# A four-layer convolution stack: expansion rows of layer 0 in four PSUM banks, with copies of 768 columns

## The chip, the cores and the metric

The kernel runs on one core of a Trainium2 chip. The metric is the device time of one execution in microseconds (us); lower is better. Times before a change and after it are medians of several runs.

## What is computed

Four layers are applied one after the other to `x` of shape (4, 64, 256, 256); each adds its result to its input, which is first group-normalized (`_gn`). Only layer 0 is touched:

```python
x = jnp.einsum('bchw,oc->bohw', x, w_in)             # 64 -> 384 channels: the "expansion"
xf = jnp.fft.rfft2(patches_of_8x8(x)) * fft_filter
x = jnp.fft.irfft2(xf, s=(8, 8))                     # back to the image layout
x = lax.conv_general_dilated(x, w_dw, ..., feature_group_count=C)   # 3x3 per channel
x1, x2 = jnp.split(x, 2, axis=1)
x = jax.nn.gelu(x1, approximate=False) * x2          # 384 -> 192
return jnp.einsum('bchw,oc->bohw', x, w_out)         # 192 -> 64: the "projection"
```

The filter and the 3x3 convolution together are one linear map for each channel, from the 64 pixels of a patch and some of its neighbours to 64 output pixels.

## The kernel before

Layer 0 works on 12 blocks `p` (three for each of four images). A block has up to 12 rows of patches; a row of patches is 8 image rows by 32 patches. Four blocks have 12 steps of expansion for each channel block, eight have 11, since the image's edge leaves a row out.

For each block a loop over four channel blocks `kb` (48 channels of each of the two halves `x1` and `x2`) does this:

1. **Expansion** (`expand`, lines 459 to 490). One step makes 16 patches of each of two rows (or one whole row). The stationary operand is the pixels, the moving one the 96 weights `win`, so that pixels come out on partitions and channels along the free dimension. If `pairs` is true, one matmul takes two patches: 128 pixels on 128 partitions, 16 matmuls a step in the program (L470). If not, each patch has a matmul of its own on 64 partitions, 32 a step (L476); the weights are then taken in such an order that the channels land on the half of the partitions where they belong. The hardware records show two matmuls for each one in the program.
2. **Copies of the expansion** into the tile `u` in SBUF (L486 for pairs, L488 to L490 for single patches). A step has two PSUM tiles of two banks each, `s` = 0 and 1. ScalarE (ACT) empties tile 0, VectorE (DVE) tile 1. Pairs need four copies of 64 partitions x 384 elements from each tile, single patches three.
3. **The convolution** (`own` L523, `beside` L539) from `u` into PSUM tiles `pc`, then GELU on ScalarE (L546), the product on VectorE (L547) and a store of `g` to DRAM. It has twelve groups `g` for a `kb`, in pairs.
4. At four of these pairs, the first among them, `unit()` does a part of the **projection** of the block before (`project`, matmuls L632 and L639, additions on VectorE L648 to L653), which comes between the last matmul of the expansion and the first of `own`.

`banks(name)` hands out PSUM: four tags of two banks each, in turn, for everything in layer 0. A step of expansion takes two of the four tags, so the matmuls of step t+2 need the tiles of step t to be empty. Pairs are used in all steps of `kb` = 0 and in the first six steps of the other three channel blocks; the rest are single patches.

TensorE, VectorE, ScalarE and the DMA queue of SyncE run in the order in which the program is written (`manual_schedule`); semaphores between engines come from the framework, which follows who writes and reads which tile.

## Time and profile before

| what | value |
|---|---|
| median of 3 runs | 6347.42 us (6346.17 to 6354.44) |
| the profiled execution | 6345.01 us, of which 6343.0 us span |
| TensorE matmul (PE) busy | 5965.4 us, 94% |
| VectorE (DVE) busy | 4315.4 us, 68% |
| ScalarE (ACT) busy | 3274.7 us, 52% |
| layer 0, from its first expansion to the first matmul of layer 1 | about 107 to 3793 us |
| granted clock of TensorE from 105 to 3792 us, mean | 0.99 |

A profile is one execution; its times are not a median. PE is a matmul, PEld a weight load that runs beside matmuls. "Idle before" is the time for which an engine stood still ahead of a group of instructions, and the arrow names what it waited for. "PEclk" is the share of the full clock that TensorE was granted. L12 is line 12 of the kernel.

### The profile page before, as it was taken

How to read it: one execution, taken by the hardware profiler on the slowest of the kernel's cores; microseconds unless marked ns; L12 is line 12 of the kernel's file. 1: busy time of each engine (PE TensorE's matmuls, PEld its weight loads, DVE VectorE, ACT ScalarE, POOL GpSimd, SP SyncE). 2: the span in 40 equal slices, each digit the busy share in tenths (PEclk: the TensorE clock that was granted, in tenths of full speed). 3: DMA queues.
4: the chain of work that ended last, by engine and by line, in shares of the span. 5: the costliest groups of instructions: out<-in, count | busy, mean ns of one | idle time of the engine just before them, and what ended most of it. 6: DMA issues, size and time to landing. Idle time of an engine off the chain costs nothing.

```text
span 6343.0 us, 233229 instructions
## 1 busy us (share of the span) xinstructions
PE 5965.4 (94%) x104150; PEld 3328.8 (52%) x104150; DVE 4315.4 (68%) x6003; ACT 3274.7 (52%) x4639; POOL 1054.2 (17%) x1651
## 2 busy tenths in 40 slices
PE   3999999999999999999999969999899999999987
PEld 2565655566665655556665533333344444443566
DVE  6566666666666666656665549999788988984265
ACT  4454444445454444344544407777777777772111
POOL 4111111111111111111111111111122222221011
PEclk9999999999999999999999979999999999999755
DMA  7477888887887878887768799999566666678799
GB/s 221 157 209 220 241 240 248 244 235 228 239 234 225 239 231 241 235 249 207 219 200 224 217 239 246 227 230 225 136 175 174 175 173 176 175 189 292 290 374 393
DMA packets 769595, 1441.98 MB, mean 227 GB/s; under 512 B 77412, under 2 KB 463476, under 8 KB 766548
## 3 DMA queue, kind: packets, MB, share of 16 engines
q1 hardware_dynamic: 616388, 917.72, 54.7%
q0 software_dynamic: 148672, 500.14, 23.5%
q8 instruction: 823, 13.48, 0.9%
q10 hardware_dynamic: 3536, 9.20, 0.6%
q14 instruction: 176, 1.44, 0.1%
HBM read 926.71 MB, written 500.04 MB: 225 GB/s over the span
## 4 chain that ended last, share of the span: by engine, by line
PE 83%; DVE 6%; DMA 6%; ACT 3%; issue 2%; POOL 0%; SPq 0%; ACTq 0%; POOLq 0%; DVEq 0%
PE pc L539 18%; PE pc L523 12%; PE m L946 10%; PE one L1187 9%; PE psu L470 8%; PE div L1146 7%; PE po L632 4%; DVE u L486 4%; PE psu L476 3%; PE psz L1176 2%; PE po L639 2%; ACT u L486 2%; PE psy L1521 2%; PE psa L1374 2%; DMA x<-x 2%
## 5 line engine op out<-in xcount | busy, mean ns | idle before, releaser
L547 DVE TENSOR_TENSOR h<-h,pc 128x374 f32<-128x374 f32 x1152 | 575.4, 541 | 1168.8 <-ACT h L546 1168.8
L546 ACT ACTIVATE h<-pc 128x374 f32<-128x374 f32 x1152 | 493.4, 480 | 1682.3 <-PE pc L539 1682.3
L539 PE MATMUL pc<-u,w 64*16 64x374 f32 (+2 forms) x27648 | 1178.0, 479 | 4.7 <-issue 4.5
L550 POOL DMA_DIRECT2D g<-h x576 | 415.5, 721 | 2834.5 <-DVE h L547 2724.2
L523 PE MATMUL pc<-u,w 64*64 64x374 f32 x9216 | 832.0, 484 | 10.1 <-DVE u L490 3.4
L486 DVE COPY u<-psu 64x384 f32<-64x384 f32 x1408 | 782.3, 556 | 60.4 <-PE psu L470 36.4
L539 PEld LDWEIGHTS pc<-u,w 64*16 64x16 f32 (+2 forms) x27648 | 465.5, 92 | 682.0 <-issue 645.4
L470 PE MATMUL psu<-win,xn 64*128 64x96 f32 x11264 | 759.9, 277 | 47.7 <-ACT u L486 26.7
L486 ACT COPY u<-psu 64x384 f32<-64x384 f32 x1408 | 722.8, 513 | 128.2 <-PE psu L470 100.8
L470 PEld LDWEIGHTS psu<-win,xn 64*128 64x128 f32 x11264 | 714.4, 188 | 114.3 <-ACT u L486 36.2
L1132 DVE TENSOR_TENSOR q<-xn 128x2313 f32<-128x2313 f32 (+2 forms) x256 | 628.0, 2495 | 1.7 <-ACT xn L253 1.7
L1187 PE MATMUL one<-z,wp 32*32 32x512 f32 x16384 | 598.1, 598 | 18.7 <-issue 14.9
L253 ACT ACTIVATE xn<-x,nb,r 128x1024 f32<-128x1024 f32 (+3 forms) x267 | 475.3, 1802 | 179.2 <-DMA x<-r 117.8
L523 PEld LDWEIGHTS pc<-u,w 64*64 64x64 f32 x9216 | 363.9, 132 | 383.5 <-issue 159.1
L1133 ACT ACTIVATE q<-q 128x2313 f32<-128x2313 f32 (+2 forms) x256 | 529.2, 2087 | 31.4 <-DVE q L1132 30.3
L1187 PEld LDWEIGHTS one<-z,wp 32*32 32x32 f32 x16384 | 368.7, 103 | 228.2 <-issue 87.7
L1146 PE MATMUL div<-q,ones 64*32 64x512 f32 x8192 | 465.9, 596 | 11.1 <-ACT q L1133 9.5
L1220 POOL DMA_DIRECT2D x<-r x512 | 274.5, 544 | 974.7 <-DVE r L1217 959.5
L476 PE MATMUL psu<-win,xn 64*64 64x96 f32 x12288 | 345.6, 250 | 39.9 <-issue 18.4
L632 PE MATMUL po<-g,wo 128*64 128x176 f32 (+1 forms) x3072 | 315.2, 348 | 45.0 <-DMA g<-g 36.9
L476 PEld LDWEIGHTS psu<-win,xn 64*64 64x64 f32 x12288 | 299.8, 135 | 82.3 <-issue 34.5
L946 PE MATMUL m<-t,wk 64*64 64x512 f32 x3072 | 341.1, 588 | 0.0
(157 smaller groups left out, 6428.7 us busy)
## 6 DMA issues: line engine op xcount, KB each, us to landing
g<-h POOLq DMA_DIRECT2D x576, 374.0 KB, 6.7
x<-x SPq DMA_DIRECT2D x240, 640.0 KB, 6.5
w<-wt SPq DMA_DIRECT2D x288, 448.0 KB, 6.9
x<-x SPq DMA_DIRECT2D x100, 1024.0 KB, 14.1
g<-g SPq DMA_DIRECT2D x414, 187.0 KB, 6.4
g<-g SPq DMA_DIRECT2D x736, 93.5 KB, 6.0
x<-in_x_dram SPq DMA_DIRECT2D x256, 256.0 KB, 8.0
x<-o POOLq DMA_DIRECT2D x128, 512.0 KB, 8.3
```

Of the source, the lines that this page charges most:

```text
L470: nc.tensor.matmul(ps[s][:, k, at], xn[halves[s], n : n + 2].rearrange("p n r w -> p (n r w)"), win[halves[s], kb, 0 : 2 * PB], start=True ...
L476: nc.tensor.matmul(ps[s][halves[1 - odd], k, at], xn[halves[s], n + odd].rearrange("p r w -> p (r w)"), win[halves[s], kb, PB * (1 - odd) ...
L486: copy(at(h, o0 + o), v[k, c : c + PB])
L523: nc.tensor.matmul(out(C * c, C, k, h), w[halves[h], k, 2 * (G % 2) + c, 0:C], cells(h, 4 * g + 2 * k + c, 0, 0), start=True, stop=False, ...
L539: nc.tensor.matmul(out(q, m, k, h), w[halves[h], k, 2 * (G % 2) + c, c0 : c0 + m], cells(h, 4 * g + 2 * k + c, down, right), start=False, ...
L547: nc.vector.tensor_mul(h[:, k], h[:, k], ps[k][:, 1, 0:L])
L632: nc.tensor.matmul(out(k, s, x), wo1, moving(g1[:, 2 * k], 2 * half + k, s, x), start=(x == 0), stop=False, skip_group_check=True,)
L946: nc.tensor.matmul(rows2(m)[halves[j], s], w[dx][halves[s]], ts[n][halves[s], i, 2 * j : 2 * j + 2, dx : dx + W], start=(dx == 0), stop=(d ...
L1132: nc.vector.tensor_sub(d, p0, p1)
L1133: nc.scalar.activation(d, d, AF.Square)
L1146: ins = nc.tensor.matmul(ps[quarters[j], h], ones[halves[h]], q[n, g, k][halves[h], r + 2 * j : r + 2 * j + 2, o : o + W], start=(m == 0), ...
L1187: ins = nc.tensor.matmul(rows2(ps[g])[quarters[j], k], w[quarters[i]], z[quarters[i], h, 2 * j + dy : 2 * j + dy + 2, dx : dx + W], tile_p ...
```

## The change

The four tags of two banks become one tile of all eight banks, `psum`, from which `banks(name, n)` hands out slices of two or four banks, aligned to their size. A step of expansion now takes one slice of four banks (two for each `s`). In each bank a group of 96 channels starts at a multiple of 128 columns, no longer of 96, so that the eight groups of an `s`, and both `s`, lie at even distances. One copy now takes both `s`: 768 elements instead of 384, half as many copies. They are dealt to the engines by kind and not by `s`: for pairs ScalarE, VectorE, ScalarE, VectorE; for single patches ScalarE, VectorE, ScalarE. All copies of a step thus read the same four banks. Last, in the channel blocks 1 to 3 pairs and single patches alternate from step to step (`t % 2 == 0`), where before pairs came first; the number of steps of each kind stays the same.

```diff
-        turn = count()
-        def banks(name):
-            return pp.tile([128, 2, 512], F32, tag=f"p{next(turn) % 4}", name=name)
+        psum = pp.tile([128, 8, 512], F32, name="psum0")
+        turn = [0]
+        def banks(name, n=2):
+            k = -(-turn[0] // n) * n % 8
+            turn[0] = k + n
+            return psum[:, k : k + n]
...
-            ps = [banks(f"psu_{p}_{kb}_{i}_{q}_{s}") for s in range(2)]
+            ps = banks(f"psu_{p}_{kb}_{i}_{q}", 4)
...
-                    n, at = 2 * (4 * k + m), slice(2 * PB * m, 2 * PB * (m + 1))
+                    n, at = 2 * (4 * k + m), slice(128 * m, 128 * m + 2 * PB)
...
-                                ps[s][:, k, at], xn[halves[s], n : n + 2].rearrange("p n r w -> p (n r w)"),
+                                ps[:, 2 * s + k, at], xn[halves[s], n : n + 2].rearrange("p n r w -> p (n r w)"),
...
-            at = lambda h, o: u[h, :, o : o + 8].rearrange("p c (s m) -> p c s m", s=2)
-            for s, copy in enumerate((nc.scalar.copy, nc.vector.tensor_copy)):
-                o0 = to[s][0] * CW + 8 * to[s][1]
-                v = ps[s][:, :, 0 : 8 * PB].rearrange("p s (m c) -> p c s m", m=4)
-                if pairs:
-                    for h, o, k, c in ((lo, O1, lo, 0), (hi, O2, lo, PB), (lo, E1 + 1, hi, 0), (hi, E2 + 1, hi, PB)):
-                        copy(at(h, o0 + o), v[k, c : c + PB])
-                    continue
-                copy(at(slice(0, 128), o0 + 1), v[:, 0:PB])
-                copy(at(hi, o0 + E2 + 1), v[lo, PB:])
-                copy(at(lo, o0 + O1), v[hi, PB:])
+            o0, o1 = (CW * t + 8 * s for t, s in to)
+            v = ps.rearrange("p b n -> p (b n)").rearrange("p (s m c) -> p c s m", s=2, m=8)
+            def copy(engine, h, o, k, c):
+                d = u[h]
+                d = bass.AP(tensor=d.tensor, offset=d.offset + o0 + o, ap=[d.ap[0], d.ap[1], [o1 - o0, 2], [1, 8]])
+                engine(d, v[k, c : c + PB])
+            act, dve = nc.scalar.copy, nc.vector.tensor_copy
+            if pairs:
+                copy(act, lo, O1, lo, 0)
+                copy(dve, lo, E1 + 1, hi, 0)
+                copy(act, hi, O2, lo, PB)
+                copy(dve, hi, E2 + 1, hi, PB)
+            else:
+                copy(act, slice(0, 128), 1, slice(0, 128), 0)
+                copy(dve, lo, O1, hi, PB)
+                copy(act, hi, E2 + 1, lo, PB)
...
-                            expand(p, kb, steps[t], kb == 0 or t < (NR + 1) // 2)
+                            expand(p, kb, steps[t], kb == 0 or t % 2 == 0)
```

More of the change, by code (lines that the diff above doesn't have):

```diff
@@ L476, in expand @@
                             nc.tensor.matmul(
-                                ps[s][halves[1 - odd], k, at], xn[halves[s], n + odd].rearrange("p r w -> p (r w)"),
+                                ps[halves[1 - odd], 2 * s + k, at], xn[halves[s], n + odd].rearrange("p r w -> p (r w)"),
                                 win[halves[s], kb, PB * (1 - odd) : PB * (3 - odd)], start=True, stop=True,
                             )
-            at = lambda h, o: u[h, :, o : o + 8].rearrange("p c (s m) -> p c s m", s=2)
-            for s, copy in enumerate((nc.scalar.copy, nc.vector.tensor_copy)):
-                o0 = to[s][0] * CW + 8 * to[s][1]
-                v = ps[s][:, :, 0 : 8 * PB].rearrange("p s (m c) -> p c s m", m=4)
-                if pairs:
-                    for h, o, k, c in ((lo, O1, lo, 0), (hi, O2, lo, PB), (lo, E1 + 1, hi, 0), (hi, E2 + 1, hi, PB)):
-                        copy(at(h, o0 + o), v[k, c : c + PB])
-                    continue
-                copy(at(slice(0, 128), o0 + 1), v[:, 0:PB])
-                copy(at(hi, o0 + E2 + 1), v[lo, PB:])
-                copy(at(lo, o0 + O1), v[hi, PB:])
+            o0, o1 = (CW * t + 8 * s for t, s in to)
[14 more added lines that the diff above has]
+                copy(act, hi, E2 + 1, lo, PB)
         def load_w(j):
```

## The prediction

> **What bounds the kernel now.** I read the page's engine shares and its chain of waits first, then its costliest groups for the expansion, then the timeline of one channel block, then windows with the granted clock.

> ```profile
> PE 5965.4 (94%) x104150; PEld 3328.8 (52%) x104150; DVE 4315.4 (68%) x6003; ACT 3274.7 (52%) x4639; POOL 1054.2 (17%) x1651
> ...
> PE 83%; DVE 6%; DMA 6%; ACT 3%; issue 2%; POOL 0%; SPq 0%; ACTq 0%; POOLq 0%; DVEq 0%
> ...
> L486 DVE COPY u<-psu 64x384 f32<-64x384 f32 x1408 | 782.3, 556 | 60.4 <-PE psu L470 36.4
> ...
> L486 ACT COPY u<-psu 64x384 f32<-64x384 f32 x1408 | 722.8, 513 | 128.2 <-PE psu L470 100.8
> ```

> TensorE bounds nearly everything; DVE and ACT are in the chain with 6% and 3%, and the chain's lines name L486 for most of that: the copies of pair steps. The timeline of one channel block (kb = 3, eleven steps) shows why:

> ```profile
> 2105.49 13.74 DVE L486 COPY u<-psu 64x384 f32<-64x384 f32 x24 [0.46 <-PE psu L470]
> 2105.50 6.43 ACT L486 COPY u<-psu 64x384 f32<-64x384 f32 x12 [1.13 <-PE psu L470]
> ...
> 2126.62 3.48 PE L476 MATMUL psu<-win,xn 64*64 64x96 f32 x128 [0.40 <-ACT u L490]
> ```

> Both engines begin together and run beside each other. Six pair steps take DVE 13.74 us, 2.29 a step; that is the pace of pair steps. The first one's matmuls took 2.01 us (a chain piece of 32 records from 2103.45), so TensorE could go faster. Two single-patch steps (128 records) take TensorE 3.48 us, 1.7 a step, and the copies 1.6 to 1.7: balanced.

> Adding up the timeline of TensorE over all 48 channel blocks, from the first matmul of an expansion to the first L523 after it (the projection's 2.4 us between them included), gives 1283.5 us: 29.3 for kb = 0 with twelve steps, 27.1 with eleven, else mostly 25 to 29.

> [...] the two engines copy at once, from different banks. [...]

> ```profile
> 595.55:598.96 3.41, 1.50 (x17) 0.46 (x14) 0.56 (x2) 0.96 (x2) 0.72 (x1) 1.00 1.02 368
> 598.96:602.37 3.41, 3.41 (x28) 1.49 (x20) 0.53 (x1) 0.00 (x0) 0.72 (x1) 0.50 1.02 287
> ...
> 2022.33:2025.74 3.41, 2.18 (x27) 0.94 (x29) 1.09 (x2) 0.96 (x2) 0.71 (x1) 1.00 1.00 370
> 2025.74:2029.15 3.41, 3.41 (x76) 1.47 (x76) 0.00 (x0) 0.00 (x0) 0.72 (x1) 1.00 1.03 355
> 3315.99:3319.40 3.41, 1.93 (x65) 1.40 (x62) 2.45 (x5) 1.91 (x4) 0.00 (x0) 1.00 0.12 20
> 3319.40:3322.82 3.42, 3.42 (x97) 3.42 (x92) 1.82 (x4) 1.91 (x4) 0.00 (x0) 0.50 0.02 5
> ```

> Columns: stretch, its length, busy time of PE, PEld, DVE, ACT and POOL, granted clock, DMA share, GB/s. A window with 1.50 or 1.93 us of PE work is followed by one at clock 0.50; one with 2.18 is not. All these stretches lie on one grid of 3.413 us. So about 1.4 us of idling inside one window costs the next window half its clock.

> **The change part by part.**

> *The waits.* All copies of a step read the same four banks of one tile. In the built program of the changed kernel the second copy of a step on ACT waits for DVE, and every one on DVE for ACT; the semaphore values resolve to the copy just before, on the other engine:

> ```
> 117 L489 TensorCopy u<-psum_90 64x48x2x8 [waits DVE_49,PE_49]
> 118 L489 TensorCopy u<-psum_90 64x48x2x8 [waits DVE_49]
> 160 L489 TensorCopy u<-psum_90 64x48x2x8 [waits Activation_49] x15
> ```

> (the first two on ACT, the third on DVE).

> So within a step the copies run one after another: A, D, A, D for pairs, A, D, A for singles. Before, no copy of one engine waited for the other. Only the last D of a pair step can run beside the first A of the next step. The first matmul of step t+2 waits for the last copy of step t. Behind the waiting copies stand only further copies; then come GELU and products, which wait for the convolution anyway.

> *Prices.* D: 384 elements take 556 ns, 512 (tm<-pst L1492) 679, so about 0.96 ns an element: 768 take 0.95 us (0.93 to 0.97). A: 384 take 480 to 530 by form; 512 (L1379) take 585 and 1024 (L1199, L1180) 1007 to 1032, 0.85 an element: 0.83 us (0.80 to 0.88). A handoff h between engines: 0.03 to 0.04 us in the chain of waits; 0.04 (up to 0.07). Matmuls: pairs 2.01, singles 1.71 us a step. The 128-column spacing is priced at nothing, the element count being equal.

> *Pace of alternating steps.* From the end of a pair step's last copy: h, 2.01 of matmuls for the next pair step, then A, D, A, D with four more h: 2.01 + 2 x 0.83 + 2 x 0.95 + 0.20 = 5.77 us for a pair and a single step. (The copies alone would need 3A + 3D + 4h = 5.50; the singles' matmuls fit in.) Before: 2.29 + 1.71 = 4.00.

> *Pace in kb = 0.* The same loop spans two pair steps: 2.885 a step, before 2.29.

> *Sums without a change of clock.* The first copy starts at 2.05 us. Eleven steps: 2.05 + 10 x 2.885 + (2A + 2D + 3h = 3.68) + 0.04 = 34.62 until L523 may start, for kb = 0 and for the alternation (five cycles and a last pair step) alike; the projection (2.41) hides in the last copies. Twelve steps of kb = 0: 37.43 (the start is not quite even). Twelve alternating: the projection needs the banks of step 10, 34.62 + 2.41 = 37.03, and the last single step hides behind it. In all 8 x 34.62 + 4 x 37.43 + 24 x 34.62 + 12 x 37.03 = 1701.9; minus 1283.5: **+418 us**. The gain that half as many fixed costs and the even mixing could bring is inside this.

> *The clock.* In an alternating cycle TensorE works 3.72 of 5.77 us and idles about 2.05 in one piece. A window that must hold 1.37 us of this starts within 3.41 + 2.05 - 2 x 1.37 = 2.72 of 5.77 us: 47% of 1.7 windows, 0.8 slow windows a cycle. The slow window begins between 0.7 us before and 2.0 after the pair step's matmuls start and lengthens them by 0 to 2.0, on average 1.05 us: 0.85 a cycle, for five such reloads in each of 36 channel blocks 153 us. In kb = 0 the usual gap is only 0.9 us, with one of 1.7 near the start: about 2 us a block, 24 in all. The pause before L523 sets the first of the convolution slow about half the time, 1.7 us lost: 48 x 0.9 = 43. Together about **+220**, from 0 (the gaps always straddle the windows) to 330 (threshold at 65% busy and copies at the upper prices).

> *Other edits.* Slices of four banks now and then skip two: at most a wait for one product, after a norm only; nothing. Convolution, GELU and product still lie in different banks and get no new waits. Later layers are untouched.

> Sum: 6345.0 + 418 + 220 = 6983; the median is 2.4 us above the profiled execution: 6985.

> **Rivals.**

> *Waits without slow clock.* For it: the 2.05-us gaps may straddle windows, one window at 53% busy in layer 0's tail stayed fast, and the records give 1.00 for the first 105 us, in which TensorE hardly works. Against: the five others below 58% in this layer's loop before all tipped. 6347 + 418 = 6765.

> *The clock stays low throughout the expansions.* Cycle 5.77 + 2.01 = 7.78; over 192 cycles and 68 pairs of kb = 0, 260 x 2.01 = 523: 6347 + 418 + 523 = 7288. Against: at half clock TensorE works 7.4 of 7.8 us, and the trace shows windows that are full at 0.50 followed by full clock.

> *The handoffs cost nothing and each engine runs its own copies freely.* Then pairs go at 2.01 (TensorE), singles at 1.71 (ACT 1.66), saving 0.28 on 352 pair steps: 6347 - 99 = 6248. It decides from the point at which a step's four copies take less than its matmuls; serial they take 3.6 us against 2.01, so only a program without these waits gives it. The built one has them.

> **How the numbers follow.** Forecast 0.72; waits alone 0.15; clock low throughout 0.09; free copies 0.04. The copies' price bounds move 418 to 390 or 490. The range reaches from just below the second case, 6730, to 7110 (clock loss 270 and upper prices), leaving out the last two cases and some of the edges. Differences under 0.2% of the time can't be told from none here: faster 0.035, same 0.01, slower 0.955.

> **What would show it.** The L489 copies on DVE idle before them, released by ACT L489, and ACT's by DVE L489, hundreds of us each; means near 0.83 and 0.95; ACT and DVE alternating in the timeline; L473 waiting for the last DVE copy; expansions of 38 to 44 us up to L533; layer 0 ending near 4430; its granted clock near 0.9. It is wrong if ACT and DVE copy at the same time, or if copies of 768 take much less than 0.8; if the clock stays at 1.00, the second case holds.

## The result, and the profile after

The changed kernel takes 6983.36 us (median of 4 runs, 6975.09 to 6989.48), the kernel before 6348.66 us in the same comparison: a ratio of 1.1002, 95% interval 1.0989 to 1.1015. It is 10% slower. The profiled execution has a span of 6977.3 us, 634.3 more than before.

The page after: engine shares, the chain of waits by engine, and the three groups of the expansion.

```profile
PE 6220.6 (89%) x104150; PEld 3587.0 (51%) x104150; DVE 4072.4 (58%) x4915; ACT 3201.2 (46%) x3743; POOL 1053.6 (15%) x1651
...
PE 74%; DVE 9%; ACT 7%; DMA 5%; issue 4%; POOL 1%; SPq 0%; ACTq 0%; POOLq 0%; DVEq 0%
...
L489 DVE COPY u<-psum 64x768 f32<-64x768 f32 x896 | 860.1, 960 | 988.9 <-ACT u L489 980.0
L489 ACT COPY u<-psum 64x768 f32<-64x768 f32 (+1 forms) x1088 | 943.8, 868 | 908.6 <-DVE u L489 575.1
L473 PE MATMUL psum<-win,xn 64*128 64x96 f32 x11264 | 934.2, 332 | 432.7 <-DVE u L489 421.9
```

The copies themselves became cheaper, since one of 768 elements takes VectorE 960 ns and two of 384 took 2 x 556: VectorE's busy time fell by 243 us, ScalarE's by 74. But VectorE now stands still for 980 us ahead of its copies, released by a copy of ScalarE, and ScalarE for 575 us, released by one of VectorE. (The 980 us include the time in which ScalarE's first copy of a step itself waits for the matmuls.) Before, neither engine's copies waited for the other's; the pair copies waited for TensorE, for some 36 and 101 us. TensorE in turn waits 422 us for VectorE's copy ahead of a pair step, and its busy time *rose* by 255 us with the same 104150 matmul records. Two costs are thus to be told apart: waiting, and slower matmuls.

The timeline after (columns: start, length, engine, line, form, count, idle before and its releaser) in an alternating channel block, and the clock in the windows of 3.413 us over the same stretch (the columns are those of the prediction's windows):

```profile
3449.61 0.89 ACT L489 COPY u<-psum 64x768 f32<-64x768 f32 x1 [1.14 <-PE psum L473]
3450.53 0.96 DVE L489 COPY u<-psum 64x768 f32<-64x768 f32 x1 [2.89 <-ACT u L489]
3451.52 1.80 ACT L489 COPY u<-psum 64x768 f32<-64x768 f32 x2 [1.03 <-DVE u L489]
3452.43 1.95 DVE L489 COPY u<-psum 64x768 f32<-64x768 f32 x2 [0.95 <-ACT u L489]
3453.45 2.73 PE L473 MATMUL psum<-win,xn 64*128 64x96 f32 x32 [1.65 <-DVE u L489]
3454.42 0.80 ACT L489 COPY u<-psum 64x768 f32<-64x768 f32 x1 [1.10 <-DVE u L489]
3456.11 2.44 PE L479 MATMUL psum<-win,xn 64*64 64x96 f32 x64
3456.27 0.89 ACT L489 COPY u<-psum 64x768 f32<-64x768 f32 x1 [1.05 <-PE psum L473]
```

```profile
3444.35:3447.76 3.41, 1.72 (x50) 1.53 (x44) 2.31 (x3) 1.86 (x3) 0.00 (x0) 1.00 0.02 5
3447.76:3451.17 3.41, 3.41 (x62) 3.24 (x64) 0.64 (x1) 1.60 (x2) 0.00 (x0) 0.50 0.00 0
3451.17:3454.59 3.42, 1.77 (x48) 1.58 (x44) 2.24 (x3) 1.95 (x3) 0.00 (x0) 1.00 0.00 0
3454.59:3458.00 3.41, 3.41 (x64) 3.24 (x66) 0.80 (x1) 1.52 (x2) 0.00 (x0) 0.50 0.02 5
3458.00:3461.42 3.42, 1.84 (x46) 1.65 (x42) 2.08 (x3) 2.10 (x3) 0.00 (x0) 1.00 0.00 0
3461.42:3464.83 3.41, 3.41 (x30) 2.73 (x28) 0.96 (x1) 1.46 (x3) 0.00 (x0) 0.50 0.00 0
```

ScalarE and VectorE take turns: each copy starts about 0.03 us after the other engine's has ended, and only a single step's first ScalarE copy runs beside a pair step's last VectorE copy (0.9 us together here, from 3452.43). These two write the same `u` but read different banks, so here a common target does not make copies wait; what the waiting ones have in common besides is the banks. The pair step's matmuls start 0.06 us after VectorE's last copy of the step two before (3452.43 + 0.96 = 3453.39). They take 2.73 us here, not 2.03 as at full clock, because the clock halves inside them, to 0.50 from 3454.59 on: in this block every other window has its pause, is busy for only 1.72 to 1.84 us, and is followed by a slow one. The cycle of a pair and a single step takes 6.75 us, from 3446.70 to 3453.45.

Few blocks look like this one. The trace has 180 cycles from one pair step's matmuls to the next pair step's, 6.57 us on average. Of these 93 took less than 6.05 us, nearly all with pair matmuls of 2.03 us; 56 took 7.25 us or more, with pair matmuls of 3.3 to 3.7 us; only 16 lie between 6.6 and 6.9. A block of the commoner kind, TensorE and the windows:

```profile
4042.53 2.03 PE L473 MATMUL psum<-win,xn 64*128 64x96 f32 x32 [2.33 <-DVE u L489]
4048.51 3.74 PE L473 MATMUL psum<-win,xn 64*128 64x96 f32 x32 [2.47 <-DVE u L489]
4052.17 2.84 PE L479 MATMUL psum<-win,xn 64*64 64x96 f32 x64
4056.19 2.03 PE L473 MATMUL psum<-win,xn 64*128 64x96 f32 x32 [1.18 <-DVE u L489]
4062.17 3.73 PE L473 MATMUL psum<-win,xn 64*128 64x96 f32 x32 [2.47 <-DVE u L489]
```

```profile
4045.08:4048.50 3.42, 0.96 (x48) 0.77 (x40) 1.93 (x3) 2.25 (x3) 0.00 (x0) 1.00 0.06 10
4048.50:4051.91 3.41, 3.40 (x32) 3.40 (x32) 0.94 (x1) 0.80 (x1) 0.00 (x0) 0.50 0.02 5
4051.91:4055.33 3.42, 3.10 (x68) 2.63 (x66) 1.11 (x2) 1.93 (x3) 0.00 (x0) 0.50 0.00 0
4055.33:4058.74 3.41, 2.55 (x60) 2.46 (x64) 1.76 (x2) 1.96 (x3) 0.00 (x0) 1.00 0.00 0
4058.74:4062.16 3.42, 0.96 (x48) 0.77 (x40) 1.93 (x3) 2.25 (x3) 0.00 (x0) 1.00 0.02 5
```

Here the window with 0.96 us of work at 4045.08 is followed by two slow ones. A fast cycle of 5.98 us and a slow one of 7.68 us together fill four windows, 13.66 us; of the 144 pairs of neighbouring cycles within a block, 41 add up to 13.6 to 13.7 us.

### The profile page after: what moved, and what is told of

The parts are those of the page before. It is cut to its first block, busy times and chain, and to the rows that moved or that the text cites. A ratio compares the mean times of both kernels' runs of the same rounds, so it can differ in the third digit from the quotient of the medians.

```text
span 6977.3 us, 230954 instructions
## 1 busy us (share of the span) xinstructions
PE 6220.6 (89%) x104150; PEld 3587.0 (51%) x104150; DVE 4072.4 (58%) x4915; ACT 3201.2 (46%) x3743; POOL 1053.6 (15%) x1651
## 3 DMA queue, kind: packets, MB, share of 16 engines
q14 instruction: 167, 1.37, 0.1%
## 4 chain that ended last, share of the span: by engine, by line
PE 74%; DVE 9%; ACT 7%; DMA 5%; issue 4%; POOL 1%; SPq 0%; ACTq 0%; POOLq 0%; DVEq 0%
PE psum L549 16%; PE psum L533 11%; PE psum L473 10%; PE m L956 9%; PE one L1197 8%; DVE u L489 7%; ACT u L489 7%; PE div L1156 6%; PE psum L642 4%; DMA x<-x 2%; PE psz L1186 2%; PE psum L649 2%; PE psa L1384 2%; PE psy L1531 1%; PE zero L1197 1%
## 5 line engine op out<-in xcount | busy, mean ns | idle before, releaser
L489 DVE COPY u<-psum 64x768 f32<-64x768 f32 x896 | 860.1, 960 | 988.9 <-ACT u L489 980.0
L489 ACT COPY u<-psum 64x768 f32<-64x768 f32 (+1 forms) x1088 | 943.8, 868 | 908.6 <-DVE u L489 575.1
L473 PE MATMUL psum<-win,xn 64*128 64x96 f32 x11264 | 934.2, 332 | 432.7 <-DVE u L489 421.9
L556 ACT ACTIVATE h<-psum 128x374 f32<-128x374 f32 x1152 | 493.6, 480 | 1688.3 <-PE psum L549 1687.9
L557 DVE TENSOR_TENSOR h<-h,psum 128x374 f32<-128x374 f32 x1152 | 575.2, 541 | 1152.1 <-ACT h L556 1151.9
L549 PE MATMUL psum<-u,w 64*16 64x374 f32 (+2 forms) x27648 | 1178.2, 479 | 0.4 <-issue 0.3
L473 PEld LDWEIGHTS psum<-win,xn 64*128 64x128 f32 x11264 | 869.6, 240 | 520.6 <-DVE u L489 478.4
L533 PE MATMUL psum<-u,w 64*64 64x374 f32 x9216 | 842.6, 485 | 17.9 <-DVE u L489 15.7
L549 PEld LDWEIGHTS psum<-u,w 64*16 64x16 f32 (+2 forms) x27648 | 469.0, 92 | 674.1 <-issue 629.5
L533 PEld LDWEIGHTS psum<-u,w 64*64 64x64 f32 x9216 | 393.4, 133 | 373.6 <-issue 201.5
L479 PE MATMUL psum<-win,xn 64*64 64x96 f32 x12288 | 401.0, 296 | 3.9 <-issue 3.9
L479 PEld LDWEIGHTS psum<-win,xn 64*64 64x64 f32 x12288 | 357.1, 171 | 29.9 <-issue 20.2
```

The lines of the kernel that those rows point to most:

```text
L473: nc.tensor.matmul(ps[:, 2 * s + k, at], xn[halves[s], n : n + 2].rearrange("p n r w -> p (n r w)"), win[halves[s], kb, 0 : 2 * PB], start ...
L479: nc.tensor.matmul(ps[halves[1 - odd], 2 * s + k, at], xn[halves[s], n + odd].rearrange("p r w -> p (r w)"), win[halves[s], kb, PB * (1 - ...
L489: engine(d, v[k, c : c + PB])
L533: nc.tensor.matmul(out(C * c, C, k, h), w[halves[h], k, 2 * (G % 2) + c, 0:C], cells(h, 4 * g + 2 * k + c, 0, 0), start=True, stop=False, ...
L549: nc.tensor.matmul(out(q, m, k, h), w[halves[h], k, 2 * (G % 2) + c, c0 : c0 + m], cells(h, 4 * g + 2 * k + c, down, right), start=False, ...
L557: nc.vector.tensor_mul(h[:, k], h[:, k], ps[k][:, 1, 0:L])
```

## The experiments

Each time is a median, each ratio is to the kernel before, measured beside it on the same chip.

**Copies dealt by `s` again.**

```diff
-                copy(act, lo, O1, lo, 0)
-                copy(dve, lo, E1 + 1, hi, 0)
...
+            for s, copy in enumerate((nc.scalar.copy, nc.vector.tensor_copy)):
+                v = ps[:, 2 * s : 2 * s + 2].rearrange("p s (m c) -> p c s m", m=4)
```

> Edit: the changed kernel with only the dealing of the copies undone: ScalarE copies the two banks of s = 0 and VectorE those of s = 1, 384 elements each, 4 or 3 copies per step and engine; the one PSUM tile of eight banks, the 128-column spacing and the alternation of pairs and single patches stay. Theory (the engines wait for each other because all copies of a step read the same four banks): the waits between the two engines' copies are gone, an alternating cycle goes at the pace of VectorE's copies, 4 x 0.556 + 3 x 0.556 = 3.9 us, and the time is back at 6300 to 6370 us with the granted clock of layer 0 at 0.99. Rival (the spacing, the single big tile or the alternation is what costs): it stays above 6800 us.

Measured: 6398.3 us, 1.0087 (1.0072 to 1.0102). The mutual waits are gone and with them nearly all of the loss. So in this program the sharing of the banks by both engines is what costs, with 1.1002 as against 1.0087. The run also goes back to copies of 384 elements, but these mean more work and not less (VectorE is busy for 4314.7 us, after the change 4072.4); copies of 768 elements without sharing were not run. In a pair step of the changed kernel ScalarE reads partitions 0 to 63 of the four banks and VectorE 64 to 127, and they wait all the same: the waits are semaphores of the program. Whether copies from the two halves could run at once was not tried, and what two engines reading one bank would do without these semaphores was not shown. But 53 us remain, which the theory had not allowed for. The timeline of this run shows where:

```profile
2132.94 1.55 PE L479 MATMUL psum<-win,xn 64*64 64x96 f32 x64
...
2135.12 2.27 PE L473 MATMUL psum<-win,xn 64*128 64x96 f32 x32 [0.63 <-ACT u L489]
...
2137.31 1.20 PE L479 MATMUL psum<-win,xn 64*64 64x96 f32 x42
```

From one single step to the next 4.37 us pass, more than the 4.00 of the kernel before. A pair step's matmuls wait for the copies of the pair step *two* before, and its own copies wait for it: about 2.1 + 2.2 us, one after the other, once in every two steps. When pairs stand together the same loop also spans two steps, but both are pairs, and it hides behind VectorE's 2 x 2.29 us.

**Pairs first again.**

```diff
-                            expand(p, kb, steps[t], kb == 0 or t % 2 == 0)
+                            expand(p, kb, steps[t], kb == 0 or t < (NR + 1) // 2)
```

> Edit: the changed kernel with only the alternation undone: in channel blocks 1 to 3 the first six steps are pairs, the rest single patches. Theory (serial copies plus half clock in the gaps): a run of single steps is paced by A + D + A + 2h = 2.8 us and leaves TensorE's clock off the critical loop, a run of pair steps goes at 2.93; the sum is 392 us above before without a loss of clock, with about 95 us of clock loss left in kb = 0 and at the start of the convolution: 6790 to 6870 us, faster than the changed kernel. Rival (the alternation is neutral or a help, the clock has no part): 6960 us or more.

Measured: 6830.3 us, 1.0771 (1.0748 to 1.0794), in the middle of what was expected. The clock of layer 0 rose from 0.90 to 0.93. The alternation costs the changed kernel 2.3 points.

**Filling the pause.** This is the sharpest test of the clock, since it adds work.

```diff
-                        for odd in range(2):
+                        for odd in (0, 1) * (1 + (4 * k + m > 1)):
```

> Edit: the changed kernel, but three quarters of the matmuls of the single-patch steps are issued twice (same operands, same place), which lengthens such a step on TensorE from 1.71 to 2.99 us and shortens its pause in a cycle from about 2.1 to 0.85 us, below the 1.4 us that tips a window. Theory (part of the loss is the half clock after the pauses): although TensorE does more work, the time falls, by about 128 us of clock loss in the alternating blocks less up to 30 us for the longer steps: 6860 to 6920 us. Rival (the whole loss is the serial copies): no fall, 6980 us if the extra work hides in the pauses, up to 7200 us (192 x 1.28 us more) if it does not.

Measured: 6920.4 us, 1.0896 (1.0871 to 1.0920). With 9216 more matmul records the kernel is 63 us faster, and the interval lies clear of the changed kernel's. The windows over layer 0 of the changed kernel and of this one:

```profile
105.00:4425.00 4320.00, 3781.02 (x66616) 2421.67 (x66620) 2010.20 (x2875) 1584.23 (x2365) 589.88 (x796) 0.90 0.68 193
```

```profile
105.00:4370.00 4265.00, 3789.82 (x75804) 2433.20 (x75804) 2004.80 (x2865) 1579.28 (x2362) 589.91 (x796) 0.95 0.69 195
```

The busy time is the same for 9188 more records, at a clock of 0.95 instead of 0.90. The clock is seen at the pair steps themselves: of the 180 that have a single and another pair step behind them, 149 now take less than 2.1 us of matmuls, in the changed kernel 93; above 2.03 us each they cost 33 us in all, in the changed kernel 110. The gain in time is at the small end of what was expected: the waits list of this run has 54 us of idling at L479 and 14 at L473 put down to issue, of which the changed kernel has 4 at L479, so that the filling seems to have made new pauses of its own.

**Two copies, then two.**

```diff
-                copy(act, lo, O1, lo, 0)
-                copy(dve, lo, E1 + 1, hi, 0)
-                copy(act, hi, O2, lo, PB)
-                copy(dve, hi, E2 + 1, hi, PB)
+                copy(act, lo, O1, lo, 0)
+                copy(act, hi, O2, lo, PB)
+                copy(dve, lo, E1 + 1, hi, 0)
+                copy(dve, hi, E2 + 1, hi, PB)
```

(and in single steps both ScalarE copies ahead of VectorE's)

> Edit: the changed kernel with the copies of a step in another order: pairs ScalarE, ScalarE, VectorE, VectorE; single patches ScalarE, ScalarE, VectorE. One handoff in a step instead of three or two, and the two engines can work on neighbouring steps. Theory (the loop that binds is matmuls of a pair step, then its four copies one after another, then the bank is free for the step after next): 2.01 + 2A + 2D + 3h = 5.8 us for two steps instead of 5.87, so only about 20 us less: 6930 to 6990 us. Rival (the handoffs and the chain from copy to copy bind): each engine's own copies set the pace, 2A = 1.74 or 2D = 1.92 us a step, and the time falls to 6350 to 6550 us.

Measured: 6979.4 us, 1.0997 (1.0981 to 1.1014): no different from the changed kernel. The number of handoffs is not what binds, nor is each engine's own share of the copies. What binds is that a step's copies stand one after another between two uses of the same banks.

**The alternation alone**, in the kernel before (the line shown for "pairs first again", the other way round).

> Edit: the kernel before with the alternation alone (pairs when t is even in channel blocks 1 to 3); four tags of two banks, 96-column spacing and copies by s as before. Theory (with two steps' worth of PSUM, a pair step's matmuls start only when the copies of the pair step two before are done: 2.01 + 2.24 + handoffs = 4.35 us for a pair and a single step, against 2.29 + 1.71 = 4.00 when pairs stand together): about 0.35 x 180 = 60 us slower than before, 6390 to 6415 us, as the run with copies by s. Rival (the 53 us of that run come from the spacing or the one big tile): 6335 to 6355 us.

Measured: 6422.1 us, 1.0140 (1.0122 to 1.0158). The rival falls: alternating is a loss of its own. At 86 us it is larger than the 60 us expected; this run has 55 us of TensorE idling put down to issue in the expansion, the kernel before 20, which accounts for the size of the difference but is not shown to be its cause.

**One tile, spacing and slices alone**: copies by `s` and pairs first.

> Edit: the changed kernel with copies by s (384 elements) and with pairs first, so that of the change only the one tile of eight banks, the slices and the 128-column spacing stay. Theory: these cost nothing, 6335 to 6360 us. Rival (they cost the 53 us): 6385 to 6410 us.

Measured: 6295.6 us, 0.9939 (0.9926 to 0.9953). Neither expectation holds: this is *faster* than the kernel before, by 40 us, and the fastest kernel of the study. The waits lists (who waited for whom, us in total, times, longest) from 105 to 3650 us name a difference, here the kernel before and then this one:

```profile
PE psu L476 <- issue: 18.4, 28, 3.1
```

```profile
PE psum L479 <- issue: 1.1, 3, 0.5
```

Pauses of up to 3 us at single steps are gone, and the expansions' sum fell from 1283.5 to 1249.4 us.

**Spacing alone**, in the kernel before.

```diff
-                    n, at = 2 * (4 * k + m), slice(2 * PB * m, 2 * PB * (m + 1))
+                    n, at = 2 * (4 * k + m), slice(128 * m, 128 * m + 2 * PB)
...
```

(and the copies' slices to match)

> Edit: the kernel before with the 128-column spacing alone; four tags of two banks, copies by s, pairs first. It tells apart what makes the version with one tile of eight banks, copies by s and pairs first about 40 us faster than before, with TensorE's pauses of issue at single steps nearly gone. If the spacing does it: 6285 to 6310 us, and the pauses gone. If the one tile and its waits do it: 6325 to 6355 us, with pauses as before.

Measured: 6335.0 us, 0.9999 (0.9991 to 1.0007): nothing. By elimination the 40 us come from the one tile, unless it takes both together; the tile alone was not run. The trace with it has 1296 separate wait instructions on TensorE, with four tags 2369. Whether fewer of them spare the pauses was not tested, and it can't be the whole reason: the last run below has the same 1296, and its pauses put down to issue at L479 are back at 52 us. The cause stays open.

**More single steps.** On the profile's durations single steps look cheaper than pairs, so two kernels tried them in the kernel before, and one in the faster version above.

> Edit: the kernel before with single patches in all steps of all channel blocks. From the profile a single step takes 1.71 us on TensorE and 1.67 on VectorE, a pair step 2.29 on VectorE: 352 pair steps x 0.57 = 200 us less, 6130 to 6170 us. Rival: single steps have twice the instructions (128 records of matmuls and weight loads in 1.7 us), and the pauses of about 3 us put down to issue, which the profile before shows at single steps, become common and tip the clock as well: 6300 us or more.

> Edit: the kernel before with pairs in the first three steps instead of six in channel blocks 1 to 3 (all pairs in the first channel block as before). 108 pair steps become single: 108 x 0.57 = 62 us less, 6275 to 6300 us. Rival (pauses of issue at single steps grow with their number): 6340 us or more.

> Edit: the version with one tile, copies by s and pairs first, with pairs in the first three steps instead of six in channel blocks 1 to 3. If it is free of the pauses whatever the number of single steps, 108 pair steps less save 0.6 us each: 6225 to 6250 us. If the pauses come back with more single steps in a row, as they did in the kernel before with three pair steps: 6300 us or more.

Measured: single steps only 6453.4 us, 1.0193 (1.0175 to 1.0210); three pair steps instead of six 6361.3 us, 1.0041 (1.0028 to 1.0055); the same in the faster version 6304.6 us, 0.9949 (0.9936 to 0.9962), no better than with six (0.9939). All three hopes fell; in the run of singles only, TensorE idles so:

```profile
PE psu L476 <- issue: 260.0, 154, 5.0
```

Its clock, averaged over the span, is 0.943 against 0.960. So pairs stay for a reason that durations of single instructions don't show.

## Why the prediction was right

*The waits.* Right in mechanism and nearly in size. The copies took 0.868 us on ScalarE and 0.960 on VectorE on average, against 0.83 and 0.95. With these the prediction's own sum for the expansions gives 2.01 + 2A + 2D + 0.20 = 5.87 us for a cycle, 35.2 us for eleven steps, and 1730 - 1283.5 = +446 us instead of +418. The shortest block of eleven pair steps measured 34.94 us. The term that was too small is mainly A, whose copies took from 799 to 907 ns. The loop at full clock was a little longer still: 59 of the 180 cycles took 5.95 to 6.0 us.

*The clock.* Right in mechanism, by the filled pause. The expansions add up to 1896.9 us, 167 above 1730; the remaining 634 - 613 = 21 us lie outside them. Together this leaves 188 us against the 220 forecast. It is a remainder, but its parts can be looked up in the trace, and they are less even than the prediction's averages: most cycles are either at full clock or about 1.3 to 1.8 us longer, and often one of each fills four windows. Nor is the share of work that tips a window sharp, as the prediction's 1.4 us of idling had it (the figures stand at the end).

*Where the clock term was mis-sized.* In the alternation the prediction had 0.85 us a cycle, 153 in all; the pair matmuls of the 180 cycles, which stand in the loop, took 110 us more than at 2.03 us each, 0.61 a cycle. For kb = 0 it took 2 us a block, 24 in all; the eleven-step blocks averaged 38.9 and the twelve-step ones 41.1 us, 3 to 4 above the sum at full clock, about 42 in all. For the start of the convolution it took 43 us; the first 128 matmuls of the 48 convolutions took 31 us more than before in sum (366 against 335), not all of which need be the clock. So the alternation and the convolution were put too high, by some 43 and 12 us, kb = 0 and the waits too low, by some 18 and 28.

*Other edits.* "Nothing" was wrong for the one tile: with the spacing it is worth -0.6% when the engines don't share banks; how much of this gain the changed kernel keeps was not separated. And the even mixing, put down as a possible gain inside the sum, is a loss: 1.4% alone in the kernel before, 2.3 points in the changed kernel. The prediction's cycle did contain the loop that makes it so, but did not draw the conclusion that pairs first would be faster in either kernel.

Steps of ratio sum up the change: one tile and spacing -0.6 points, shared banks with serial copies +8.3 (0.9939 to 1.0771), alternation on top +2.3 (1.0771 to 1.1002). That the total came out within 2 us of the forecast owes something to the opposite errors above.

*Rivals.* Waits without a slow clock fell with the windows at 0.50; a clock that stays low throughout fell as well, since the mean cycle is 6.57 us and not 7.78, and layer 0 ran at 0.90 (the argument against it, that a full window at half clock is followed by full clock, holds only in part: 45 of the 102 slow stretches of layer 0 last two windows, 38 last one); free copies fell with the 980 and 575 us of mutual waiting.

## What to carry to other kernels

Where the program makes the copies of two engines from the same PSUM banks wait for each other, as here, give each engine banks of its own to empty: copies half as many and twice as long took 243 us of work off VectorE, but with banks shared and copies taking turns the kernel lost 8.3 points (0.9939 to 1.0771). Before alternating light and heavy steps, follow the buffer's loop: with room for two steps, step t+2 meets step t, so that alternation pairs heavy with heavy (4.37 us for a pair and a single step with copies by `s`, 4.00 in the kernel before). Where a change opens regular pauses on TensorE, look at the clock in windows of 3.413 us, the grid on which it changed in both traces: pauses of 1.6 to 2.5 us were enough here to stretch the next pair step's matmuls from 2.03 us to as much as 3.74.

## What the runs showed of the hardware

With single steps only, so with 64 matmul records in every step, TensorE had 154 pauses at L476 that the profile puts down to issue, of up to 5.0 us and 260 us in all; in the kernel before it had 28, of up to 3.1 us and 18.4 us in all.
